# A third buffer for the masked tables, one fewer for the tables and the limits

## The chip, the cores and the metric

The kernel runs on one core of one Trainium2 chip. The metric is the device time of one execution in microseconds (us). An execution covers four graph layers over a batch of 16 graphs of 1,024 nodes with 64 channels.

The engines are named as in the profile: PE (matrix products), DVE (elementwise and reductions), ACT (activations and copies), POOL (here mostly an issuer of transfers) and SP (an issuer of transfers).

## The reference

Every layer is `x = layernorm(x + layer(x, adj))`. What each layer does, cut to what matters:

```python
# layer 0: batch norm over all nodes, then a degree-scaled propagation
Hn = batchnorm(x); d = adj.sum(2)
out0 = leaky_relu(X - sqrt(d) * (adj @ (rsqrt(d) * X)))        # X = Hn @ W + b
# layer 1: 8-head attention; scores = g0 * q.k + g1 * adj; softmax; projection
# layer 2: per node and channel, quantiles over the node's neighbours
adj_  = adj with a unit diagonal
rem   = every second neighbour in node order, of nodes with more than 10 (made symmetric)
nd    = (adj_ > 0) & ~rem                                       # [node, neighbour]
s     = sort over neighbours of where(nd, x, inf)               # per channel
nv    = nd.sum
for tau, w in ((.25, .25), (.5, .5), (.75, .25)):
    pos = tau * (nv - 1); lo, hi = floor(pos), ceil(pos)
    agg += w * (s[lo] + (pos - lo) * (s[hi] - s[lo]))
out2 = relu((x + agg) @ W1 + b1) @ W2 + b2, times a node mask
# layer 3: adj @ (x @ W) + b
```

## The kernel before

The graphs go in pairs, and the outer loop over `p` runs nine times. Round `p` does, in this order:

1. layer 0 of pair `p` (`layer0`, `neighbours`), interleaved with the end of layer 2 and the whole of layer 3 of pair `p-2` (`ends`, `layers23`);
2. attention of pair `p` (`attention`), 64 steps, with the sort of the channels of pair `p-1` beside it (`sorted_words`, from step `BESIDE = 58` on at the latest). At steps 60 to 63 (`TABLES`) `tables(2)` lets DVE make up to two tables `E`, until `EB` of them exist (`first_elements`);
3. the quantile lookup of pair `p-1` (`quantiles`). It takes more than half of the time, and most of the change is in it.

**The lookup.** Each graph has 16 groups of four channels (`G`) and three quantiles (`NQ`). That makes 96 steps for a pair: step `i` is one (graph, group, quantile). Eight steps are a unit (`U8N = 8`). This text writes "step i" for the loop variable `i`, and "the first step of a unit" for `i` divisible by 8. Per group, two tables `E` (bfloat16, 2 KB a partition each) are made by DVE (`words`, `element`), multiplied on PE with the neighbour matrix `ndT` in two halves each (`half_word`), and left by ACT as packed words in `V`. Then, per step:

- `compare(i + 2)`: DVE compares the words with the limits of the quantile (`lim`), result `lt`;
- `one_hot(i + 1)`: PE forms differences of `lt` along the ranks (`lt,dif`), ACT copies them into `oh`;
- `pick(i, 0)` and `pick(i, 1)`: DVE multiplies `V` with `oh` into a masked table `m`, 6 KB a partition. These are the "first pick" and "second pick" of a step;
- `summed(i - 1)`: twelve PE products add the two masked tables of the step before into `wps`. Both are read to nearly the last of the twelve. At the end of a unit, ACT copies `wps` into `wb`, and DVE searches the bit in it over the next six steps (`kth_bit`);
- `distances`, `least_values`, `sum_values` for the step 14 earlier: PE products, which ACT evicts into `vals`, and PE sums into `acc`;
- `more_words` and `more_elements`: the next half words on PE and the next tables on DVE. `more_elements` makes a table only if `made + 1 <= used // 2 + EB`.

**What sets the order.** PE's products of the lookup are chained in the order of the code (`product`, `in_sequence`), and so are DVE's operations that go through `v` (`InOrder`). For everything else a planner of the framework orders each engine's instructions when the program is made, by its own estimate of when inputs and buffers are free. `behind(i)` asks that an instruction be planned after the last `pick`; it is an order in that plan and no wait on the chip. A tile with `bufs=n` waits on the chip until the n-th tile before it has been read for the last time.

**Limits and weights.** `rank_limits` makes `counts` (node degrees `cnt`), `limits(q)` and `weights(t)` of a graph. For the first graph of a pair this is done ahead of the loop. For the second, `SECOND` gives the steps: counts at 26 and 28, weights at 30, 38 and 47, limits at 40, 45 and 46. A limit is one ACT operation (L717) and two DVE operations (L719); a limit of the first graph is last read by `compare` at steps 43, 44 and 45. A weight takes ACT's `kc` (L727) and `nvc` (L728, one buffer) and DVE's L731, L732, L734.

**Memory.** The tables and `lt`, `nvc`, `kc` lie in the pool `qm` at the right end of the on-chip memory; `lim`, `V`, `m` in `qe`, and then `qn`, at the left. The tiles of `layers23` (`tof`, `x2b`, `oT2`, `agg2`) lie in `agg0` at the right end, after the lookup is over.

All of DVE's `v` operations have the profile's line L749 and all chained PE products L933, since a helper records them. They are told apart by their tiles.

Of the kernel before, what the change touches and what calls it, by code (L numbers as in the profile page):

```python
# [13 lines left out]
F32 = mybir.dt.float32  # L14
F16 = mybir.dt.float16
BF = mybir.dt.bfloat16
# [9 lines left out]
P = 128  # L26
N = 1024
# [5 lines left out]
NW = 3  # L33
# [11 lines left out]
MORE = (1, 2, 1, 2, 1, 2, 1, 1)  # L45
SC = 2048.0
VB = 4
EB = 7
LB = 4
LTB = 2  # L50
SECOND = (26, 28, 30, 38, 40, 45, 46, 47)
BESIDE = 58
TABLES = (60, 61, 62, 63)
AHEAD = (10, 12, 15)
# [67 lines left out]
def gnn_kernel(ctx: ExitStack, tc: tile.TileContext, a: dict, out: bass.AP):  # L122
# [105 lines left out]
    def bank(shape, dtype=F32):  # L228
        return ps1.tile(shape, dtype, name="bank")
# [24 lines left out]
    def banks(shape):  # L254
        return two[-1].tile(shape, F32, name="banks")
# [3 lines left out]
    NODES = [P, 4, 2, C]  # L259
# [6 lines left out]
    def over_c(x):  # L266
        return by_half(x)[:, :, :, None].to_broadcast(NODES)

    def over_nodes(x):
        return x[:, None, None, :].to_broadcast(NODES)  # L270
# [25 lines left out]
    def layernorm(dst, y):  # L296

        tiles = norm_tiles()
        norm_stats(tiles, y, range(4))
        norm_apply(tiles, dst, y)  # L300

    def transposed(dst, src, then=lambda i: None):
        ps = bank([P, 512])
        for k in range(4):
            then(nc.tensor.transpose(ps[:, k * P:(k + 1) * P], src[:, k].rearrange("p f c -> p (f c)"), ident))
        nc.scalar.copy(dst, ps)
# [110 lines left out]
    def node_mask(ip, bb):  # L417
        mu = small.tile([P, NB], U8, name="mu", bufs=4)
        nc.sync.dma_start(mu, mask2d[ds(ip * (2 * P) + bb * P, P), :])
        mask_f = small.tile([P, NB], F32, name="mask_f", bufs=4)  # L420
        nc.vector.tensor_copy(mask_f, mu)
        return mask_f
# [276 lines left out]
    def rank_limits(gr, qe, qn, qm, behind):  # L699
# [14 lines left out]
        def limits(q):  # L714

            lim = gr.lim[q] = qe.tile([P, 2, N], U16, name="lim", bufs=LB)
            behind(nc.scalar.activation(lim[:, 0], cnt, AF.Copy, scale=0.25 * (q + 1), bias=-0.25 * (q + 1) - 0.375))  # L717
# [118 lines left out]
    def words(v, pool, g, w, rk, u_w, b_w):  # L836


        sh = [P, 2 * NB, T, 2]
        E = pool.tile([P, NB, P], BF, name="E", bufs=EB)  # L840
        Ev = E.rearrange("p j (h t c) -> p (j h) t c", h=2, t=T)
# [24 lines left out]
    def element(v, qm, gr, g, w):  # L866

        for half, E in enumerate(words(v, qm, gr.bb * G + g, w, rk, u_w, b_w)):
            if not half:
                gr.E.setdefault(g, []).append(E)  # L870
            yield

    def first_elements(qm, graphs):

        for n in range(EB):
            for _ in element(nc.vector, qm, graphs[0], n // EW, n % EW):
# [3 lines left out]
    def quantiles(ip, rk, u_w, b_w, qm, graphs):  # L880
# [12 lines left out]
        with ExitStack() as es:  # L893

            kb, qe, qn = [es.enter_context(tc.tile_pool(name=name, bufs=1, reuse_waits="tile"))
                          for name in ("kb", "qe", "qn")]
            psw = es.enter_context(tc.tile_pool(name="psw", bufs=1, space=PSUM, reuse_waits="tile"))

            def load_matrix(gr):
                gr.ndT = qe.tile([P, NB, N], F8, name="ndT", bufs=2)  # L900
                for k in range(NB):
                    nc.sync.dma_start(gr.ndT[:, k, :].bitcast(U8), nd_d[gr.bb][ds(ip * P, P), k, :])
                gr.bv = qe.tile([P, G, 1], F16, name="bv", bufs=2)
                for c4 in range(4):
                    nc.gpsimd.dma_start(gr.bv[of_channel(c4)],
                                        scratchb[gr.r].rearrange("(g k) (t u) -> k t g u", k=4, u=1)[c4])
# [62 lines left out]
            def pick(u, s, kk):  # L969
                gr, g, q = u.pairs[s]  # L970
                nonlocal picked
                m = qe.tile([P, NW, N], BF, name="m", bufs=2)
                picked = v.tensor_tensor(m, gr.V[g].bitcast(BF),
                                         u.oh[s][:, kk, None, :].to_broadcast([P, NW, N]), ALU.mult)
                u.m.append(m)
# [92 lines left out]
            todo = [(k, w) for k in range(len(groups)) for w in range(EW)]  # L1068
            made, used = EB, 0
            del todo[:made]  # L1070

            def elements():

                nonlocal made
                k, w = todo.pop(0)
                made += 1
                yield from element(v, qm, *groups[k], w)
# [5 lines left out]
            def more_elements(n):  # L1083
                for _ in range(n):
                    if todo and made + 1 <= used // 2 + EB:
                        yield from elements()
# [29 lines left out]
            for i, (u, s) in enumerate(steps):  # L1116
                if i == 3 * NQ:
                    load_matrix(graphs[1])
                if i == SECOND[0]:
                    counts, limits, weights = rank_limits(graphs[1], qe, qn, qm, behind)  # L1120
                if i in SECOND:
                    part, n = ((counts, 0), (counts, 1), (weights, 0), (weights, 1),
                               (limits, 0), (limits, 1), (limits, 2), (weights, 2))[SECOND.index(i)]
                    part(n)
# [61 lines left out]

    hidden = []

    def layers23(agg0, agg1, agg2, tof, ip, bb):
        row = ip * (2 * N) + bb * N  # L1190
        x2 = agg0.tile(NODES, F32, name="x2b")
        oT = agg0.tile([P, 512], F32, name="oT2")
        for f in range(2):
            nc.sync.dma_start(x2[:, :, f, :], x2_d[ds(ip * P, P), 4 * f:4 * f + 4, bb, :])
            nc.sync.dma_start(oT[HALF[f]], x2T_d[ds(ip * P + bb * C, C), f * 512:(f + 1) * 512])
        mask_f = node_mask(ip, bb)
        agg = agg0.tile([P, NU, 512], F32, name="agg2")
        i = nc.scalar.dma_start(agg, agg_d[bb])
        if bb:
            tc.add_manual_dep(i.ins, hidden[0].ins.name, in_order, reason="after the first graph's")  # L1200
        pa = bank([P, 512])
        for u in range(NU):
            for f in range(2):
                nc.tensor.matmul(pa[HALF[f]], tof[HALF[f], u, :], agg[HALF[f], u, :], start=(u == 0),
                                 stop=(u == NU - 1), tile_position=(f * C, f * C))
        nc.vector.tensor_tensor(oT, pa, oT, ALU.add)
        yield
        hp = banks([P, 2, 512])
        hT = agg1.tile([P, N], F32, name="hT", bufs=1)
        for f in range(2):  # L1210
            nc.tensor.matmul(hp[:, f], w1[HALF[f]], oT[HALF[f]], start=True, stop=True)
        hidden[:] = [nc.scalar.activation(hT, hp.rearrange("p f n -> p (f n)"), AF.Relu, bias=b1)]
        yield
        py = bank(NODES)
        for k in range(NB):
            nc.tensor.matmul(py[:, k % 4, k // 4, :], hT[:, k * P:(k + 1) * P], w2, start=True, stop=True)
        y = agg1.tile(NODES, F32, name="y2", bufs=1)
        nc.vector.tensor_tensor(y, py, over_nodes(b2_r), ALU.add)
        nc.vector.tensor_tensor(y, y, over_c(mask_f), ALU.mult)
        nc.vector.tensor_tensor(y, y, x2, ALU.add)  # L1220
        yield
        x3 = agg1.tile(NODES, F32, name="x3")
        layernorm(x3, y)
        yield

        x3T = agg1.tile([P, 512], F32, name="x3T")
        transposed(x3T, x3)
        sup = agg1.tile(NODES, F32, name="sup", bufs=1)
        nc.scalar.copy(sup, by_weights(x3T, w3, C))
        yield  # L1230
        zp = bank([P, 512])
        for k in range(NB):
            at = agg2.tile([P, N], F32, name="at3", bufs=3)
            nc.sync.dma_start(at, adjT2d[ds(row + k * P, P), :])
            propagate(zp, sup, at, k)
            yield
        zT = agg1.tile([P, 512], F32, name="x3T")
        nc.scalar.copy(zT, zp)
        zn = untransposed(zT)
        nc.vector.tensor_tensor(y, zn, over_nodes(b3_r), ALU.add)  # L1240
        nc.vector.tensor_tensor(y, y, x3, ALU.add)
        yield
        layernorm(x3, y)
        for f in range(2):
            nc.sync.dma_start(node_rows(out2d, row, f), x3[:, :, f, :])
# [115 lines left out]
    def ends(ip):  # L1361

        with (tc.tile_pool(name="agg0", bufs=1, reuse_waits="tile", side="right") as agg0,
              tc.tile_pool(name="agg1", bufs=2, reuse_waits="tile", side="right") as agg1,
              tc.tile_pool(name="agg2", bufs=1, reuse_waits="tile", side="right") as agg2):
            tof = agg0.tile([P, NU, C], F32, name="tof")
            nc.scalar.dma_start(tof, a["c_tof"])
            for bb in range(2):
                yield from layers23(agg0, agg1, agg2, tof, ip, bb)

    for p in range(B // 2 + 1):
# [17 lines left out]
        with double_banks(), ExitStack() as es:  # L1391
            last = ends(p - 2) if p >= 2 else iter(())
            if p < B // 2:
                own2 = es.enter_context(tc.tile_pool(name="own2", bufs=1, reuse_waits="tile"))
                x2 = own2.tile([P, NB, 2, C], F32, name="x2")
# [38 lines left out]
            else:  # L1434
                sorted_words()
                tables_of(EB)
        if p >= 1:
# [35 lines left out]
```

## Time and profile before

| What | us |
| --- | --- |
| median of 3 runs | 11,837.91 |
| lowest and highest | 11,832.29 and 11,863.36 |
| the profiled execution's own time | 11,843.83 |
| its span in the trace | 11,842.1 |
| PE busy | 10,550.8 (89%) |
| DVE busy | 10,276.8 (87%) |
| ACT busy | 7,468.6 (63%) |
| POOL busy | 712.4 (6%) |

The mean granted clock of PE in that execution was 0.958. The span runs from the first instruction of the trace to the last; 1.7 us of the profiled time lie outside it. Shares are averages over stages that have different limits. In a group of instructions the columns are: line, engine, operation, out<-in by the program's names, shapes, count; then busy time, mean ns of one, and idle time of the engine just before them with what ended it.

### The profile page before, as it was taken

How to read it: one execution, taken by the hardware profiler on the slowest of the kernel's cores; microseconds unless marked ns; L12 is line 12 of the kernel's file. 1: busy time of each engine (PE TensorE's matmuls, PEld its weight loads, DVE VectorE, ACT ScalarE, POOL GpSimd, SP SyncE). 2: the span in 40 equal slices, each digit the busy share in tenths (PEclk: the TensorE clock that was granted, in tenths of full speed). 3: DMA queues.
4: the chain of work that ended last, by engine and by line, in shares of the span. 5: the costliest groups of instructions: out<-in, count | busy, mean ns of one | idle time of the engine just before them, and what ended most of it. 6: DMA issues, size and time to landing. Idle time of an engine off the chain costs nothing.

```text
span 11842.1 us, 207662 instructions
## 1 busy us (share of the span) xinstructions
PE 10550.8 (89%) x81864; PEld 4573.6 (39%) x82560; DVE 10276.8 (87%) x18374; ACT 7468.6 (63%) x13812; POOL 712.4 (6%) x1212
## 2 busy tenths in 40 slices
PE   7989898998989989898898998989889998983897
PEld 4645232552335423354233542335322453221232
DVE  3588998889988899788997889988999889998996
ACT  5766666666666666566665666656666566661664
POOL 0010000000000000000000000010000100001000
PEclk8989999999999999999999999999999999996999
DMA  2021002210032000310004100041000410002001
GB/s 87 25 100 42 6 6 95 80 29 4 5 110 69 24 4 6 130 52 21 5 6 138 46 18 6 6 143 43 16 5 16 139 43 10 8 24 89 4 5 50
DMA packets 310001, 508.98 MB, mean 43 GB/s; under 512 B 120480, under 2 KB 220192, under 8 KB 306976
## 3 DMA queue, kind: packets, MB, share of 16 engines
q1 hardware_dynamic: 225296, 309.02, 8.3%
q0 software_dynamic: 50688, 99.75, 2.6%
q10 hardware_dynamic: 33040, 86.88, 2.2%
q8 instruction: 649, 10.63, 0.4%
q14 instruction: 328, 2.69, 0.1%
HBM read 379.03 MB, written 116.46 MB: 42 GB/s over the span
## 4 chain that ended last, share of the span: by engine, by line
PE 56%; DVE 27%; ACT 8%; issue 5%; DMA 3%; ACTq 0%; SPq 0%; DVEq 0%; POOL 0%
PE bank L933 19%; DVE m L749 8%; PE banks L549 7%; PE bank L571 7%; PE bank L585 7%; PE acc L933 5%; PE wps L933 3%; DVE S L749 3%; DVE lt L749 3%; ACT vals L1027 2%; DVE U L749 2%; DVE wb L749 2%; PE bank L414 1%; DVE key L1285 1%; PE bank L528 1%
## 5 line engine op out<-in xcount | busy, mean ns | idle before, releaser
L749 DVE TENSOR_TENSOR m<-V,oh 128x3072 bf16<-128x3072 bf16 x1536 | 2671.1, 1750 | 252.0 <-PE wps L933 219.1
L1027 ACT ACTIVATE vals<-bank 128x512 f32<-128x512 f32 x2848 | 1470.5, 602 | 1016.3 <-PE bank L933 1003.1
L933 PE MATMUL bank<-ndT,E 128*128 128x512 fp8e4 x7936 | 1942.2, 389 | 0.0
L556 DVE CUSTOM_DVE_ANT_0 s<-banks,adj 128x1024 f32<-128x1024 f32 x1024 | 1214.0, 1220 | 521.6 <-PE banks L549 516.4
L967 ACT CAST oh<-bank 128x512 f16<-128x512 f32 x3072 | 1591.0, 617 | 20.2 <-PE bank L933 18.6
L575 ACT COPY pT<-bank 128x512 f32<-128x512 f32 x1536 | 802.4, 593 | 812.2 <-PE bank L571 812.1
L564 ACT ACTIVATE s<-s,mx 128x1024 f32<-128x1024 f32 x1024 | 1176.4, 1160 | 98.6 <-DVE mx L556 95.9
L933 PEld LDWEIGHTS <-E 128*128 128x128 bf16 x7936 | 707.8, 99 | 1228.2 <-issue 551.2
L549 PE MATMUL banks<-kT,qT 64*128 64x512 f32 x4096 | 1113.0, 628 | 74.1 <-DVE mx L556 48.5
L571 PEld LDWEIGHTS bank<-ident,s 128*128 128x128 f32 x8192 | 900.6, 143 | 417.8 <-issue 289.7
L571 PE MATMUL bank<-ident,s 128*128 128x128 f32 x8192 | 1034.8, 280 | 8.4 <-ACT s L564 8.1
L933 PE MATMUL bank<-lt,dif 128*128 128x512 bf16 x2424 | 787.4, 383 | 262.9 <-issue 81.4
L585 PE MATMUL bank<-pT,v 128*64 128x256 f32 x8192 | 1003.8, 388 | 0.0
L749 DVE TENSOR_TENSOR lt<-V,lim 128x2048 bf16<-128x2048 uint16 x768 | 934.5, 1217 | 0.0
L933 PE MATMUL wps<-m,tonesb 128*32 128x512 bf16 x9216 | 660.8, 390 | 210.5 <-DVE m L749 208.2
L933 PE MATMUL bank<-oh,bd 64*64 64x512 f16 x11616 | 804.5, 388 | 0.0
L933 PE MATMUL acc<-vals,bonesf 128*32 128x512 f32 x5696 | 801.7, 611 | 2.2 <-ACT vals L1027 2.2
L585 PEld LDWEIGHTS bank<-pT,v 128*64 128x64 f32 x8192 | 548.1, 137 | 312.3 <-issue 47.9
L947 ACT ACTIVATE V<-bank 128x512 uint16<-128x512 f32 x512 | 305.4, 596 | 540.8 <-PE bank L933 476.8
L951 ACT ACTIVATE V<-bank 128x512 uint16<-128x512 f32 x512 | 305.5, 597 | 534.6 <-PE bank L933 533.9
L549 PEld LDWEIGHTS banks<-kT,qT 64*128 64x128 f32 x4096 | 400.1, 190 | 548.7 <-issue 341.2
L933 PE MATMUL bank<-r,pen 32*128 32x512 f16 x5808 | 587.4, 387 | 21.1 <-ACT vals L1027 13.1
(259 smaller groups left out, 14574.6 us busy)
## 6 DMA issues: line engine op xcount, KB each, us to landing
at<-in_adjT SPq DMA_DIRECT2D x256, 512.0 KB, 5.8
masks_d<-mask POOLq DMA_DIRECT2D x440, 128.0 KB, 2.0
mask<-masks_d SPq DMA_DIRECT2D x440, 128.0 KB, 2.1
adj<-in_adj SPq DMA_DIRECT2D x96, 512.0 KB, 6.0
ad<-in_adj ACTq DMA_DIRECT2D x64, 512.0 KB, 7.0
agg_d<-vals POOLq DMA_DIRECT2D x96, 256.0 KB, 2.3
agg<-agg_d ACTq DMA_DIRECT2D x16, 1536.0 KB, 7.6
nd_d<-nd SPq DMA_DIRECT2D x128, 128.0 KB, 2.1
```

The source lines that it names most:

```text
L549: then(nc.tensor.matmul(ss[h][:, hf * 512:(hf + 1) * 512], gr.qk[hp, 0][HALF[h], k * P:(k + 1) * P], gr.qk[hp, 1][HALF[h], hf * 512:(hf + ...
L556: last = nc.vector.tensor_tensor_reduce(s, ss[h], gr.adj[k], -1.0, 3.0e38, ALU.add, ALU.min, mx)
L564: then_act(nc.scalar.activation(s, s, AF.Exp, bias=mx, scale=-1.0, accum_out=sm))
L571: then(nc.tensor.transpose(ps[:, m, :], exps[h][0][:, (4 * mh + m) * P:(4 * mh + m + 1) * P], ident))
L575: then_act(nc.scalar.copy(dst, ps))
L585: then(nc.tensor.matmul(po[HALF[h]], gr.v[:, 4 * mh + m, (2 * hp + h) * C:(2 * hp + h + 1) * C], pT[h][mh][:, m, :], start=(mh == 0 and m ...
L749: i = getattr(nc.vector, name)(*args, **kw)
L933: then(nc.tensor.matmul(*args, **kw))
L947: nc.scalar.activation(gr.V[g][:, 0, cols], ps, AF.Copy, scale=2.0 ** -6, bias=OFF - MAGIC[0] / 64 - 63 / 128)
L951: nc.scalar.activation(gr.V[g][:, 2, cols], ps, AF.Copy, scale=2.0 ** -8, bias=OFF - MAGIC[1] / 256 - 255 / 512)
L967: nc.scalar.copy(u.oh[s][:, kk, cols], ps)
L1027: last = nc.scalar.activation(vals[t], ys[t], AF.Relu)
```

## The change

The masked tables `m` get a third buffer (6 KB a partition more). The tables `E` go from seven buffers to six, and the limits `lim` from four to three (2 KB and 4 KB less). `EB` also bounds how many tables are made ahead. The first limit of the second graph is asked for at step 44 in place of 40. In `ends`, the residual of layer 2 (`x2b`) is allotted ahead of `tof` in place of after it; for the second graph of a pair it is allotted where it was.

```diff
-EB = 7
-LB = 4
+EB = 6
+LB = 3
 LTB = 2
-SECOND = (26, 28, 30, 38, 40, 45, 46, 47)
+SECOND = (26, 28, 30, 38, 44, 45, 46, 47)
...
-                m = qe.tile([P, NW, N], BF, name="m", bufs=2)
+                m = qe.tile([P, NW, N], BF, name="m", bufs=3)
...
-    def layers23(agg0, agg1, agg2, tof, ip, bb):
+    def layers23(agg0, agg1, agg2, x2, tof, ip, bb):
         row = ip * (2 * N) + bb * N
-        x2 = agg0.tile(NODES, F32, name="x2b")
         oT = agg0.tile([P, 512], F32, name="oT2")
...
+            x2b = agg0.tile(NODES, F32, name="x2b")
             tof = agg0.tile([P, NU, C], F32, name="tof")
             nc.scalar.dma_start(tof, a["c_tof"])
             for bb in range(2):
-                yield from layers23(agg0, agg1, agg2, tof, ip, bb)
+                yield from layers23(agg0, agg1, agg2, agg0.tile(NODES, F32, name="x2b") if bb else x2b, tof, ip, bb)
```

## The prediction

> **What bounds it now.** I read the page's busy shares, the busy time by stretch of the second pair's lookup, its waits, then its timeline.
>
> ```profile
> PE 10550.8 (89%) x81864; PEld 4573.6 (39%) x82560; DVE 10276.8 (87%) x18374; ACT 7468.6 (63%) x13812; POOL 712.4 (6%) x1212
> ```
> ```profile
> 2624.00:3407.00 783.00, 695.20 (x5819) 231.94 (x5899) 746.37 (x1089) 519.90 (x989) 40.67 (x75) 0.98 0.02 6
> ```
> ```profile
> 2877.00:2951.00 74.00, 63.58 (x535) 20.91 (x543) 67.49 (x103) 48.80 (x92) 4.86 (x9) 0.95 0.02 6
> 2951.00:3019.00 68.00, 60.27 (x543) 19.92 (x542) 66.77 (x100) 48.23 (x91) 0.56 (x1) 1.00 0.02 5
> 3019.00:3090.00 71.00, 66.75 (x586) 22.34 (x593) 68.92 (x105) 49.40 (x94) 4.88 (x9) 1.00 0.03 6
> ```
>
> Columns: PE, PEld, DVE, ACT, POOL busy, PE's granted clock, DMA. The eight lookups (8 x 783 = 6,264 us) are over half of the span, and DVE works 746.4 of 783 us: a pair can win 36.6 us there at most. The lower rows are three units (steps 32, 40, 48 and on): from step 40 DVE is idle 1 to 2 us a unit.
>
> ```profile
> PE wps L933 <- DVE m L749: 25.6, 21, 6.0
> DVE m L749 <- PE wps L933: 24.2, 17, 4.1
> ACT nvc L728 <- DVE vals L731: 12.6, 3, 6.4
> PE bank L933 <- ACT V L949: 10.4, 8, 5.9
> PE bank L933 <- ACT V L953: 9.0, 8, 4.8
> ACT lim L717 <- DVE lt L749: 2.9, 1, 2.9
> ```
>
> Columns: total, times, longest. The second row is what a third `m` is for. By the timeline, idle time before a pick is 31.4 us a pair, always a first pick: steps 0 (2.03, on ACT's `oh`, stays), 2 (0.46), 26 (0.44), 28 (1.48), 30 to 32 (4.08, 1.76, 1.56), 38 to 40 (3.91, 1.50, 1.02), 56 (1.32), 64 (0.93), 80 (1.32), 86 to 88 (1.06, 3.08, 2.63), 95 (2.18), small rest. But DVE and PE wait for each other in turn, so it matters which of these waits the end passes through.
>
> **The third buffer.** With two, pick (i, 0) waits for sums i-1; with three, pick (i, 1) does, one pick later (1.75 us; 1.67 start to start). At a unit's first step a second wait lies right behind the pick:
>
> ```profile
> 2951.54 1.76 DVE L749 TENSOR_TENSOR m<-V,oh 128x3072 bf16<-128x3072 bf16 x1 [1.02 <-PE wps L933]
> 2953.22 0.42 DVE L749 TENSOR_SCALAR wb<-wb 128x1024 uint16<-128x1024 uint16 x1
> ```
> ```profile
> 2951.61 1.51 ACT L770 CAST wb<-wps 128x1536 bf16<-128x1536 f32 x1
> ```
>
> Sums 39 end at 2951.43, ACT copies until 2953.12, and DVE's search reads the copy at 2953.22. An earlier pick leaves DVE waiting for `wb` until the same moment. So the waits at 30 to 32, 38 to 40, 56, 64, 80 and 86 to 88 run into a wait of the same length: gain 0. At 95 PE ends its sums later than the pick asks for: 0. What remains is step 2 (0.46; PE waits for DVE in steps 6 to 13) and 26 with 28 (1.92): DVE then reaches L731 of step 30's weights earlier, and ACT stands still for that:
>
> ```profile
> 2847.56 2.07 ACT L1027 ACTIVATE vals<-bank 128x512 f32<-128x512 f32 x4
> 2854.94 0.72 ACT L728 ACTIVATE nvc<-cnt,qrow 64x512 f16<-64x512 f16 x1 [5.31 <-DVE vals L731]
> 2855.57 0.57 ACT L951 ACTIVATE V<-bank 128x512 uint16<-128x512 f32 x1
> ```
>
> This `nvc` belongs to step 38's weights; the planner put it ahead of step 29's `V`, and PE idles 4.82 us for that `V`. All of it moves by 1.92. Sum: 0.46 + 1.92 = 2.4 us a pair, 19 in all.
>
> The Trainium skill's page "Perfetto Trace Analysis", section "Optimization Strategy", says that the same gap repeating on the engine that should be saturated can mean too few buffers. By that rule all 31.4 us would go, 8 x 31.4 = 251, and the time would be 11,587. I go by the steps: 21 picks of 192 wait, in clumps that start elsewhere.
>
> **Six tables.** The code's own counts give the same number of tables in each step, one index behind, until step 81; step 82 makes one more (0.68 + 0.68), hidden by step 87's wait of 3.08 (without that cover 8 x 1.36 = 11). The least lead of made over used tables before that falls from 4 to 3. One table (0.68 + 0.42) leaves the end of attention: at 2581.20 it delays a score pass, for which ACT idles 0.67 and PE 0.38. I take 0.4 x 7 = 3 us gained (bounds 0 and 8 x 1.10 = 9).
>
> **Three limits.** Here the change adds a wait on ACT:
>
> ```profile
> 2985.23 2.07 ACT L1027 ACTIVATE vals<-bank 128x512 f32<-128x512 f32 x4 [0.57 <-PE bank L933]
> 2988.12 0.60 ACT L951 ACTIVATE V<-bank 128x512 uint16<-128x512 f32 x1 [0.82 <-PE bank L933]
> 2989.08 2.07 ACT L967 CAST oh<-bank 128x512 f16<-128x512 f32 x4
> 2994.01 1.06 ACT L717 ACTIVATE lim<-cnt 128x1024 uint16<-128x1024 f16 x1 [2.85 <-DVE lt L749]
> 2994.97 1.55 ACT L1027 ACTIVATE vals<-bank 128x512 f32<-128x512 f32 x3
> ```
>
> That is step 46's limit, waiting for `compare` of step 44. With three buffers each limit (44, 45, 46) waits for the `compare` of the step just before it, and it stands in ACT's order earlier than in the code (this one is ahead of step 45's evictions; the `nvc` above sits right behind the DVE operation that frees its buffer). I therefore place each behind the planner's estimate of that `compare`: between evictions and `V` of steps 43, 44, 45. Behind it are queued `V` and the copies `oh`; PE's last `lt,dif` product and its sums wait for `V`, DVE's picks for `oh`.
> - Step 43: evictions end 2980.4, `compare` 2982.84, limit 2984.0; `V` was 2980.68. Sums 43: +3.0.
> - Step 44: `compare` ends 2993.98 (DVE is unmoved), limit 2995.1; `V` was 2988.12. Sums 44: 2991.37 to 2997.4, +6.1.
> - Step 45: oh-copies let `compare` end 0.4 later, 3002.7; limit 3003.8, where the moved `V` would be at 3002.0. Sums 45: 3002.7 to 3008.7, +6.0 (the old stall of 2.26 is part of the old time).
> - Steps 46, 47: PE is at full pace and wins back about 1. Step 48 is a unit's first step: DVE waits for `wb`, 5.0 late.
>
> So +5.0 x 8 = 40. Bounds: +1 a pair if the limits stay behind the `oh` copies, where `compare` is nearly done (one run of 1.06); +10 if they stand ahead of evictions, so that each holds PE up as `nvc` does (4.82 and 5.92, three times, less 2.26 and the slack that steps 45 to 47 have). DVE's two L719 (0.42 each), moved from a waiting step 40 to 44, are inside. 5 is nearest to the rows.
>
> **The residual.** `x2b` was issued on SP at 1974.27 and is first read at 2043.12; 5.1 us to land leave 64 of cover. 0. If its new place is free only after the tail's last products (2028), it still lands in time, ahead of two loads for layers 3 and 0 on SP: at most +1 x 7. `tof` is needed at 2027.4.
>
> **Sum:** -19 - 3 + 40 + 0 = +18. The profiled execution took 11,843.83 (span 11,842.1 + 1.7): 11,862. It lies 5.9 above the median of 11,837.91; against the median, 11,856. A measurement of this kernel can tell about 0.3% (35.5 us) from no change; +18 is below that.
>
> **Rivals.**
> - *The wait goes and nothing takes its place.* For it: 24.2 us in the row above, DVE the busiest engine. Against: the `wb` row. With half of the 29.4 us that aren't step 0's: 11,838 - 118 + 40 - 3 = 11,757. Chance 0.11, faster.
> - *The limits stay behind the `oh` copies.* +1 for +5: 11,838 - 22 + 8 = 11,824. For it: the row at 2994.01. Against: `nvc`. Chance 0.13, same.
> - *Slower: the limits stop ACT ahead of evictions at steps 43 to 45.* +10 a pair: 11,838 - 22 + 80 = 11,896. It decides from 35.5/8 + 2.8 = 7.2 us a pair on. For it: `nvc`'s 5.31 and 6.40 with one freed buffer each. Against: by then each step's evictions are mostly issued. Chance 0.22.
> - *`x2b` holds SP's queue ahead of the loads of `adj` at 1985.85* until 2028: up to 42 x 7 = 294, 12,132. Chance 0.03.
>
> **How the numbers follow.** My own case has 0.51, of which 0.08 (limits at 7 and more) lies above 0.3%. Faster 0.11; same 0.43 + 0.13 = 0.56; slower 0.08 + 0.22 + 0.03 = 0.33. The range 11,800 to 11,925 takes in the second and third rival and the bounds of limits and tables; outside are the first (0.11), `x2b` (0.03) and about 0.05 of tails.
>
> **What would show it.** Right: idle time before first picks falls to step 0's, second picks at 30, 31, 38, 39 wait about 2 less, and DVE's `wb` at 32, 40, 56, 64, 80 waits for ACT's copy, which it doesn't now; three limits a pair wait for `lt`, about 2.4, 3.7 and 1.7 us; the unit of steps 40 to 47 is some 5 us longer, that of 24 to 31 some 2 shorter, the others alike. Wrong: a loop shorter than 775 (first rival), limits that wait under 1 us or units past 48 that change, or a tail that grows between 1972 and 2045.

## The result, and the profile after

The changed kernel took 11,890.14 us (median of 5 runs, 11,882.49 to 11,901.33) where the kernel before took 11,848.47 beside it (5 runs, 11,832.29 to 11,863.36). The ratio is 1.0036, 95% interval 1.0022 to 1.0051: 0.36% slower, inside the range, 34 us from the forecast (41.7 us more than the kernel before, where +18 was forecast). The prediction's own bound for a change that can be told was 0.3%; this lies just beyond it, on the side to which it gave 0.33. The steps of the forecast don't get the credit for the number: two large errors went against each other, and that they nearly cancelled was luck.

First the busy shares of the page after, then the same stretches as before (second pair's lookup; units of steps 32, 40 and 48). Columns as in the prediction.

```profile
PE 10566.1 (89%) x81864; PEld 4593.9 (39%) x82560; DVE 10284.6 (86%) x18374; ACT 7469.7 (63%) x13812; POOL 710.8 (6%) x1212
```
```profile
2644.00:3420.00 776.00, 692.97 (x5816) 230.81 (x5895) 747.97 (x1091) 519.34 (x987) 40.62 (x75) 0.98 0.03 6
2889.00:2962.00 73.00, 64.66 (x543) 21.12 (x547) 66.83 (x101) 48.47 (x93) 4.84 (x9) 0.95 0.02 6
2962.00:3034.00 72.00, 62.09 (x542) 20.23 (x546) 67.87 (x103) 49.02 (x92) 0.56 (x1) 0.98 0.02 5
3034.00:3100.00 66.00, 62.08 (x547) 20.60 (x551) 64.34 (x97) 45.39 (x88) 4.87 (x9) 1.00 0.03 6
```

The work is the same; the lookup is 7 us shorter (776 for 783), and of the units only that of steps 40 to 47 is clearly longer (72 for 68). The row of steps 48 and on that the prediction showed, 71.00, is no whole unit: it runs 5 us past its end. That unit took 66.0 us before (first pick to first pick, 3019.00 to 3084.99), and it does now. The profiled execution as a whole is 57.4 us longer (span 11,899.5 against 11,842.1). Split at the picks and at attention's first and last score products, from the starts in the two traces:

| Stretch | before | after | sum of differences |
| --- | --- | --- | --- |
| lookup, first to last pick, mean of 8 | 782.9 | 776.2 | -53.4 |
| last pick to the next attention, mean of 6 | 201.1 | 218.7 | +105.9 |
| attention, first to last score product, mean of 6 | 411.0 | 410.9 | -0.5 |
| end of attention to first pick, mean of 6 | 44.3 | 43.4 | -5.4 |
| start to the first pick of all | 1187.8 | 1196.2 | +8.4 |
| stretch before the last lookup | 314.2 | 311.0 | -3.2 |
| last pick to the end | 138.8 | 144.4 | +5.6 |

So the lookup won 53 us, where I had a loss of 21 (-19 for the third buffer, +40 for the limits), and the stretch *between* lookups lost 106, where I had 0. The one-time rows need no cause: the start lies between 1187.2 and 1196.2 in the profiles of all twelve kernels of this study, in no order that follows their changes.

**Inside the lookup.** The waits of the second pair's lookup (total, times, longest):

```profile
DVE m L749 <- ACT oh L967: 17.6, 11, 3.5
ACT lim L717 <- DVE lt L749: 6.6, 3, 3.7
ACT nvc L728 <- DVE vals L731: 4.8, 3, 3.9
DVE wb L749 <- ACT wb L770: 4.0, 7, 0.6
DVE m L749 <- PE wps L933: 0.5, 1, 0.5
```

The wait for which the third `m` was built is gone (24.2 to 0.5), and a part of it has moved to `oh` and to `wb`. `lim` grew from 2.9 to 6.6, `nvc` fell from 12.6 to 4.8. ACT at step 29, the place that the prediction showed:

```profile
2866.09 2.07 ACT L1027 ACTIVATE vals<-bank 128x512 f32<-128x512 f32 x4
2868.98 0.60 ACT L951 ACTIVATE V<-bank 128x512 uint16<-128x512 f32 x1 [0.82 <-PE bank L933]
2869.47 0.58 ACT L953 COPY V<-bank 128x512 uint8<-128x512 uint8 x1
2869.94 2.08 ACT L967 CAST oh<-bank 128x512 f16<-128x512 f32 x4
2872.66 1.45 ACT L728 ACTIVATE nvc<-cnt,qrow 64x512 f16<-64x512 f16 x2 [0.65 <-DVE vals L731]
```

Before, `nvc` stood between `vals` and `V` and waited 5.31. Now the planner has it behind `V` and `oh`, and it waits 0.65. Mean over the pairs, step 29 is 4.0 us shorter, step 37 as well, step 27 1.6.

**Between lookups.** SP's, ACT's and PE's rows after the first lookup, whose last pick ends at 1973.82:

```profile
2031.05 0.38 SPq L1193 DMA_DIRECT2D x2b<-x_d  x1
```
```profile
2035.90 0.33 ACTq L1367 DMA_DIRECT2D tof<-in_c_tof  x1
2036.27 0.45 ACTq L1197 DMA_DIRECT2D agg<-agg_d  x1
```
```profile
2048.80 7.96 PE L1203 MATMUL bank<-agg,tof 64*64 64x512 f32 x24 [11.92 <-DMA agg<-agg_d]
```

The same before, where the last pick ended at 1971.96:

```profile
1973.94 0.34 ACTq L1367 DMA_DIRECT2D tof<-in_c_tof  x1
1976.73 0.34 ACTq L1198 DMA_DIRECT2D agg<-agg_d  x1
```
```profile
2027.40 1.07 PE L1204 MATMUL bank<-agg,tof 64*64 64x512 f32 x2
```

Before, the loads left 2.0 and 4.8 us after the last pick, and the first two of these products ran within the tail (in which the `distances` of the last 14 steps follow). Now the loads leave 62 us after it, behind the tail's last evictions on ACT, and PE stands 11.9 us for `agg`; the first graph's whole chain of layers 2 and 3, with layer 0 of the next pair beside it, starts later.

### The profile page after: what moved, and what is told of

Same layout as the page of the kernel before. It is cut to its first block, busy times and chain, and to the rows that moved or that the text cites. A ratio compares the mean times of both kernels' runs of the same rounds, so it can differ in the third digit from the quotient of the medians.

```text
span 11899.5 us, 206953 instructions
## 1 busy us (share of the span) xinstructions
PE 10566.1 (89%) x81864; PEld 4593.9 (39%) x82560; DVE 10284.6 (86%) x18374; ACT 7469.7 (63%) x13812; POOL 710.8 (6%) x1212
## 4 chain that ended last, share of the span: by engine, by line
PE 55%; DVE 27%; ACT 8%; issue 7%; DMA 4%; POOL 0%; ACTq 0%; SPq 0%; DVEq 0%; POOLq 0%
PE bank L933 18%; PE banks L549 7%; DVE m L749 7%; PE bank L571 7%; PE bank L585 7%; PE acc L933 4%; DVE lt L749 3%; PE wps L933 3%; DVE S L749 3%; ACT vals L1027 2%; DVE U L749 2%; DVE wb L749 2%; DMA at<-in_adjT 2%; PE bank L414 1%; DVE E L749 1%
```

## The experiments

Theory A had two halves. *Addresses:* by the tiles' sizes, the left pools grow by 6 - 4 = 2 KB. In the program's memory plan `r64` (of the bit search's result), the last of them, ended before the change at byte 198,272 of a partition, and `agg0` starts at 199,136; 2,048 more bring `r64` to 200,320, which is 1,184 bytes into `agg0`. The tail reads `r64` to its last `distances`, so what lies there is late. *Order:* the third buffer wins by moving `nvc` on ACT, and the limits take back some 4 us a pair. The rivals are in the expectations. "Stretch" is the time from the last pick to the next attention, mean of six; "lookup" is the mean of eight. Ratios are to the kernel before in the same series (median 11,840.94, 11,841.76 and 11,848.28 for e1 to e4, e5 to e8, e9 and e10).

**e1, the residual's move alone.**

```diff
 (kernel before)
-    def layers23(agg0, agg1, agg2, tof, ip, bb):
+    def layers23(agg0, agg1, agg2, x2, tof, ip, bb):
...
-        x2 = agg0.tile(NODES, F32, name="x2b")
         oT = agg0.tile([P, 512], F32, name="oT2")
...
+            x2b = agg0.tile(NODES, F32, name="x2b")
             tof = agg0.tile([P, NU, C], F32, name="tof")
...
-                yield from layers23(agg0, agg1, agg2, tof, ip, bb)
+                yield from layers23(agg0, agg1, agg2, agg0.tile(NODES, F32, name="x2b") if bb else x2b, tof, ip, bb)
```

> The kernel before with only the residual of layer 2 (x2b) allotted ahead of tof. In the changed kernel a pair's lookup is about 7 us shorter than before (775.9 against 782.9, first to last pick), yet the stretch from the end of a lookup to the next attention is 17.6 us longer (218.7 against 201.1, mean of six pairs). Theory A (addresses): that stretch grows because the left pools end 2 KB further up, so that x2b, now lowest in its pool, lies over the buffers of r64, which the lookup's tail reads to its end. Here the left pools end where they did before: 0 us, the stretch stays at 201 and the time at 11,848. Theory B (order): the moved x2b by itself holds back tof and agg: the stretch is 218, and 6 x 17.6 = 106 us are added, 11,950.

Measured: 11,842.59, ratio 1.0002 (0.9993 to 1.0011); stretch 199.4, lookup 783.0. The move costs nothing by itself; theory B falls.

**e2, the change without the third buffer.**

```diff
 (changed kernel)
-                m = qe.tile([P, NW, N], BF, name="m", bufs=3)
+                m = qe.tile([P, NW, N], BF, name="m", bufs=2)
```

> The changed kernel with two masked tables in place of three (tables, limits and residual stay changed). Theory A: the left pools then end below x2b, so the stretch between lookups is 201 as before. The third buffer is what shortened steps 29 and 37 (4.0 us each, the wait of ACT's nvc for DVE's L731 with PE idle behind it), so both stalls are back, and the unit of steps 40 to 47 keeps its loss of about 4.1 from the limits: lookup 783 + 4 = 787, time 11,848 + 8 x 4 = 11,880. Theory C: the shorter steps 29 and 37 come from the fewer tables or the later limits and not from the third buffer: lookup 776, time 11,848 - 55 = 11,793. Theory B: stretch 218 and time 11,880 + 106 = 11,986.

Measured: 11,917.64, ratio 1.0058 (1.0046 to 1.0070); lookup 787.1 as expected, stretch 210.1 where I expected 201. The `nvc` row of its waits, over the whole execution, against 99.1 before and 38.5 after:

```profile
ACT nvc L728 <- DVE vals L731: 101.3, 23, 6.6
```

So it is the third buffer that moved `nvc`: C falls. But the stretch was a miss. SP's rows after the first lookup (last pick 1983.56) show the next overlap:

```profile
1987.91 18.99 SPq L448 DMA_DIRECT2D adj<-in_adj  x7
2008.99 40.47 SPq L347 DMA_DIRECT2D at<-in_adjT  x3
```

Of the three loads of `at` for layer 0, which before were issued 1.9, 4.6 and 6.1 us after that pick, the first now comes after 25 and the other two after 65. Three limits and two masked tables put `vals` 4 KB *lower*, at byte 102,624, under `at`'s third buffer (101,280 to 105,376); the tail uses `vals` to its end. That it is this tile is read from the plan and the late loads; e5 shows only that it is the addresses.

**e3, the collision taken away.** `cnt` (2 KB, last read in the middle of a lookup) gets the last place on the left, above `r64`:

```diff
 (changed kernel)
-            kb, qe, qn = [es.enter_context(tc.tile_pool(name=name, bufs=1, reuse_waits="tile"))
-                          for name in ("kb", "qe", "qn")]
+            kb, qe, qn, qc = [es.enter_context(tc.tile_pool(name=name, bufs=1, reuse_waits="tile"))
+                              for name in ("kb", "qe", "qn", "qc")]
...
-        cnt = qe.tile([P, N], F16, name="cnt")
+        cnt = qc.tile([P, N], F16, name="cnt")
...
```

> The changed kernel with one tile elsewhere: cnt (2 KB, last read before the middle of a lookup) gets a pool of its own above r64, so that x2b lies over cnt and no longer over r64; tables, limits, masked tables and the order of allotment are the changed kernel's. Theory A: the stretch from a lookup to the next attention falls from 218.7 to 201, tof and agg are issued soon after the last pick, and the lookup stays at 776: 11,890 - (6 x 17.6 + 8) = 11,777, or 11,848 - 55 = 11,793 worked out from the kernel before. Theory B (the residual's place, whatever lies under it): stretch 218, time 11,890.

Measured: 11,793.31, ratio 0.9952 (0.9940 to 0.9965); stretch 201.9, lookup 776.4. The loads are back to 3.3 and 6.1 us after the last pick (1971.96):

```profile
1975.26 0.35 ACTq L1367 DMA_DIRECT2D tof<-in_c_tof  x1
1978.05 0.34 ACTq L1197 DMA_DIRECT2D agg<-agg_d  x1
```

Every operation is the changed kernel's, and `x2b` is where it was; `cnt` lies under it in place of `r64`, and `V`, `lim`, `m` and `qn` are 2 KB lower. The other loads of that stretch weren't late in the change: `at` and `adj` left 3.3 to 21 us after the last pick, here 3.3 to 25. That settles the stretch: what lies under `x2b` decides 6 x 16.8 = 101 of its 106 us, the price of 1,184 bytes.

**e4, two buffers for `nvc`.**

```diff
 (kernel before)
-            nvc = qm.tile([P, 512], F16, name="nvc")
+            nvc = qm.tile([P, 512], F16, name="nvc", bufs=2)
```

> The kernel before with two buffers in place of one for nvc, the small tile for which ACT stands still at steps 29 and 37; nothing else changed. As planned, the weights of step 38 then need no wait and those of step 47 are asked for at step 29 in their place: the stall at step 29 should stay, the one at step 37 go. Theory A (what the third masked table won it won by moving nvc behind V on ACT): step 37 is 4 us shorter and step 29 is not, lookup 783 - 4 = 779, time 11,848 - 32 = 11,816. Theory D (the win belongs to DVE's picks, and the nvc stall is only where PE shows it): other waits fill the place, lookup 782 to 783, time 11,848.

Measured: 11,801.95, ratio 0.9963 (0.9949 to 0.9976); lookup 777.6. Step 37 is 4.0 us shorter, steps 38 and 39 together 2.1, and step 47 is 0.7 longer; step 29 is unchanged, with the stall where it was:

```profile
2859.57 0.72 ACT L728 ACTIVATE nvc<-cnt,qrow 64x512 f16<-64x512 f16 x1 [5.32 <-DVE vals L731]
2860.20 0.57 ACT L951 ACTIVATE V<-bank 128x512 uint16<-128x512 f32 x1
```

One run holds both the step that was mended and its control. Little refilled the place (0.7 at step 47, 0.5 in the last unit); D falls.

**e5, e2 with `vals`, `oh`, `r64` and what lies between at their addresses of before.**

```diff
 (e2)
+            unused = qe.tile([P, 2048], F16, name="unused")
+            nc.gpsimd.memset(unused[:, 0:2], 0.0)
             load_matrix(graphs[0])
```

> The kernel with two masked tables, six tables and three limits (e2_two_m) with an unused tile of 4 KB at the start of qe, so that vals, oh, r64 and all behind them lie where they lay in the kernel before. In e2_two_m the lookup was 788 us as expected, but the stretch to the next attention was 210 and not 201; there vals (read through the tail) had moved down 4 KB under layer 0's buffers at, whose second load came 65 us after the last pick and not 5. Theory A (addresses, this time vals under at): with the padding the stretch is 201, the lookup still 4 to 5 us over the one before: 11,841 + 8 x 4.5 = 11,877. Theory E (fewer tables or limits make the stretch longer in some other way): stretch 210, time 11,918.

Measured: 11,859.52, ratio 1.0013 (1.0004 to 1.0022); stretch 198.4, lookup 787.0. An unused 4 KB makes the kernel 58 us faster than e2, and E falls. This is also what six tables and three limits cost without the third buffer: 4.1 us a pair in the lookup (steps 43, 45 and 47: +0.8, +2.3, +1.2), 18 us in all. I expected 36; the stretch is 2.7 us shorter than before, and the profiles of kernels that are alike there lie between 199.4 (e1) and 201.9 (e3), so most of that is their spread.

**e6, the change with the residual back behind `tof`.**

```diff
 (changed kernel)
-    def layers23(agg0, agg1, agg2, x2, tof, ip, bb):
+    def layers23(agg0, agg1, agg2, tof, ip, bb):
         row = ip * (2 * N) + bb * N
+        x2 = agg0.tile(NODES, F32, name="x2b")
...
-            x2b = agg0.tile(NODES, F32, name="x2b")
             tof = agg0.tile([P, NU, C], F32, name="tof")
...
-                yield from layers23(agg0, agg1, agg2, agg0.tile(NODES, F32, name="x2b") if bb else x2b, tof, ip, bb)
+                yield from layers23(agg0, agg1, agg2, tof, ip, bb)
```

> The changed kernel with the residual (x2b) back behind tof, as before; masked tables, tables and limits stay changed. Theory A (addresses): the lowest 2 KB of the pool still lie over r64's last buffer, now with tof in it, and tof, agg and x2b are still issued only after the tail: stretch 218, lookup 776, time 11,890. Theory B (the residual's move costs the stretch): 201 and 11,793. A third outcome, x2b's move having helped: stretch above 219 and time above 11,900.

Measured: 11,877.12, ratio 1.0025 (1.0016 to 1.0034); stretch 217.2, lookup 776.3. Now `tof` itself lies over `r64`, and PE's wait is nearly as long as with `x2b` there (10.0 for 11.9), though `x2b` was issued at 1992.10:

```profile
2042.14 8.22 PE L1204 MATMUL bank<-agg,tof 64*64 64x512 f32 x24 [10.03 <-DMA agg<-agg_d]
```

The residual's place neither causes the loss nor cures it. The intervals of this kernel and of the change overlap.

**e7, three buffers for `nvc`.**

```diff
 (kernel before)
-EB = 7
+EB = 6
...
-            nvc = qm.tile([P, 512], F16, name="nvc")
+            nvc = qm.tile([P, 512], F16, name="nvc", bufs=3)
```

> The kernel before with three buffers for nvc, so that neither step 29 nor step 37 has an nvc behind DVE's L731, and six tables to make room; two masked tables and four limits as before. Two buffers (e4_two_nvc) took 4.0 us off step 37 and 2.1 off steps 38 and 39, 5.7 a pair at the end. Theory A: the stall at step 29 gives as much: lookup 783 - 11.5 = 771, time 11,841 - 8 x 11.5 = 11,749; six tables cost nothing. Theory D (waits refill elsewhere, or six tables hold PE up): no better than two buffers, lookup 777, time 11,802.

Measured: 11,724.49, ratio 0.9898 (0.9885 to 0.9912); lookup 770.9, stretch 199.6. Both stalls are gone, and six tables cost nothing that shows. The time is 25 lower than expected; the lookups explain 8 x 12.0 = 96 of the 117; of the rest, 6 x 1.5 lies between lookups and 6 x 1.7 in attention, both within what these vary by between profiles of kernels that are alike there (199.4 to 201.9 and 409.1 to 412.0).

**e8, the limits (and the last weights) one step later**, on e3:

```diff
 (e3)
-SECOND = (26, 28, 30, 38, 44, 45, 46, 47)
+SECOND = (26, 28, 30, 38, 45, 46, 47, 48)
```

> e3_counts_last (the changed kernel with the collision at the boundary taken away) with the second graph's limits asked for at steps 45, 46 and 47 in place of 44, 45 and 46, and its last weights at 48. Each limit is then asked for one step after the compare that frees its buffer, in place of in the same step. Theory A (the unit of steps 40 to 47 is 4.1 us longer because ACT stands at a limit for that compare): the unit loses under 1 us, time 11,793 - 8 x 4 = 11,761. Theory F (DVE's part of the limits, or the order around them, costs it): unit still 3 to 5 us longer, time 11,793 or more.

Measured: 11,750.60, ratio 0.9922 (0.9909 to 0.9936); lookup 772.2. The unit of steps 40 to 47 is 0.8 us longer than before, in place of 4.1, and one limit of three still waits:

```profile
2970.30 1.06 ACT L717 ACTIVATE lim<-cnt 128x1024 uint16<-128x1024 f16 x1
2979.96 1.06 ACT L717 ACTIVATE lim<-cnt 128x1024 uint16<-128x1024 f16 x1 [2.25 <-DVE lt L749]
```

F falls: 3.3 of the 4.1 us were ACT's waits at the limits.

**e9, `nvc` planned one set of weights later, no buffer changed.**

```diff
 (kernel before)
-                nc.scalar.activation(nvc[b], x, AF.Identity, bias=qrow[b, t, 4:5])
+                behind(nc.scalar.activation(nvc[b], x, AF.Identity, bias=qrow[b, t, 4:5]))
```

> The kernel before with one word changed in weights: nvc, like kc beside it, is planned behind the last pick (behind), so that ACT makes it at the step that asks for it (30, 38, 47) and not one set of weights ahead, in front of V, where it stands for DVE's L731. No buffer is added or taken, every address is that of before. Theory A (the order of nvc and V on ACT is what steps 29 and 37 lose): both stalls go as with three nvc buffers (lookup 12.3 us shorter, 11,724 measured there), less 0.7 for an nvc that now stands beside kc at each of steps 29 and 37: lookup 783 - 11 = 772, time 11,842 - 8 x 11 = 11,754 or up to 30 lower. Theory D (buffers and what is made ahead of need): steps 29 and 37 as before, 11,842.

Measured: 11,767.13, ratio 0.9934 (0.9919 to 0.9948); lookup 772.6. ACT at step 29 has no `nvc` between `vals` and `V` any more:

```profile
2842.88 2.06 ACT L1027 ACTIVATE vals<-bank 128x512 f32<-128x512 f32 x4
2845.77 0.60 ACT L951 ACTIVATE V<-bank 128x512 uint16<-128x512 f32 x1 [0.82 <-PE bank L933]
```

With every address and every count of buffers as before, an order on ACT alone is worth 10.3 us a pair: more than all that the change won in the lookup.

**e10, all of it**: e8 with e9's line.

> e8_limits_later (third masked table, six tables, three limits one step later, cnt on top) with nvc planned behind the last pick as in e9_nvc_behind. Beside e9_nvc_behind this tells what the third masked table is worth once it is not needed to move nvc. If what it wins by itself is the first units (1.2 us by step 24) and the few first picks late in a pair (steps 85, 86, 94: up to 3), less what the limits still cost: 3 us a pair, 24 us below e9_nvc_behind. If all it won was nvc's place: equal to e9_nvc_behind within 10 us. If all 31.4 - 16 = 15 us of idle time before picks counted: 120 us below.

Measured: 11,724.86, ratio 0.9895 (0.9883 to 0.9908); lookup 768.4, the shortest of all, 4.2 below e9's. The waits of the second pair's lookup:

```profile
PE wps L933 <- DVE m L749: 23.8, 21, 6.0
DVE m L749 <- ACT oh L967: 11.0, 8, 2.8
DVE wb L749 <- ACT wb L770: 3.1, 6, 0.6
```

The lookups account for 34 of the 42 us to e9. As a whole it ties with e7, which has two masked tables and nothing moved at the boundary (0.9898): either is some 120 us faster than the kernel before and 165 faster than the change.

## Why the prediction was right in its number and wrong in its steps

- **The residual: 0, bounds +1 x 7.** This step failed, and it is the largest term: +106. I followed `x2b`, and for `x2b` alone the reasoning holds (it landed at 2033 to 2035 and is read at 2066). What I didn't follow is the address. I added up what the buffers cost on the left (+6 - 4 KB) nowhere, although the change named those sizes, so I didn't see that something must then lie over `r64`. And the prediction gave `tof` and `agg` no term at all (it says of `tof` only when it is needed); both stood on ACT behind the tail's last evictions where `x2b` or `tof` lay over `r64` (the change, e6), and not where `x2b` lay over `cnt` (e3). Why the planner puts them there isn't shown: a rule that what is allotted later also comes later doesn't fit e6, where `x2b`, allotted behind the late `tof`, left 39 us ahead of it. The rival that I had for this place (`x2b` holding up SP's loads of `adj`) had the right place and the wrong victim (and its 12,132 leaves out the +18 of the other terms): `adj` was issued from 1978.6 on, and `agg` was late.
- **The third buffer: -2.4 a pair.** The first place was right (step 29), the mechanism there wasn't, and the size is wrong by a factor of over four: the change less e5 is 776.2 - 787.0 = -10.8 a pair, 86 us. I had found the row (`nvc` ahead of `V`, PE idle 4.82) and let "all of it move by 1.92", as if ACT's order were fixed. It isn't: with the third buffer the planner puts `nvc` behind `V`, and without it (e2) the stalls are back; that its estimates moved with the earlier pick is the likely reason, and not shown. What I had as a shift was a removal. The unit of steps 24 to 31 is 6.2 shorter for the forecast 2, that of steps 32 to 39 1.8 for none. With `nvc` out of the way (e10 less e9) the third buffer, with what the limits and the six tables still cost in it, is worth 4.2 a pair. The forecast 2.4 is the right order of size for that, but not its places: 2.4 of the 4.2 lie in the units from step 48 on, where I had 0.
- **The waits that I set to 0.** Right in part. Over the whole execution DVE's wait for ACT's `wb` went from 27.5 us in 8 places to 70.9 in 65, as forecast for the first steps of units. Wrong in that these waits are shorter than those that went (0.56 each in the second pair) and that the units from step 48 on are together 1.5 shorter for the forecast 0; and in that idle time before first picks did not fall to step 0's: 31.5 to 18.2 a pair, since `oh` became the late one. Second picks, which by the forecast should have come to wait, do so once in the second pair (0.46, step 46).
- **The limits: +5.0 a pair.** Right: +4.1 in the unit of steps 40 to 47 in the change, +4.6 in e5, and e8 took 3.3 of the 4.1 away. The waits came as 3.7, 1.75 and 1.1 (6.6 in all) for the forecast 2.4, 3.7 and 1.7. In step 43 the limit stood among the evictions, not behind them; the third rival's order occurred once in three, without its price. No term rests on the row of steps 48 and on that was taken for a unit.
- **Six tables: -3 in all.** The stretch from attention to the first pick is 0.9 shorter (5.4 in six); within the bounds of 0 to 1.10 each.
- **The rule.** The Trainium skill, "Perfetto Trace Analysis", section "Optimization Strategy", says that a gap that repeats on the engine that should be saturated can mean too few buffers. Read so, the gap before the picks would have been worth 251 us. The buffer alone won 86, more than half of it through `nvc` (10.8 a pair, of which e10 less e9 leaves 4.2, or by estimate some 5 with the limits' 0.8 added). Too few buffers would describe `nvc` too, whose stall repeats in every pair and which a second and third buffer removed (e4, e7), though it sits on ACT, busy 63%; and e9 removed it without any buffer.

Of what I had named as signs of error, "a tail that grows between 1972 and 2045" is what came; "a loop shorter than 775" just didn't (776.2), and no unit from step 48 on changed by more than 0.6.

The first rival had the right sign for the lookup: at other addresses the change is faster (e3: 11,793), though 36 us short of that rival's 11,757, and more than half of the gain came through `nvc`, which that rival doesn't name.

## What to carry to other kernels

When buffer counts change, add up the bytes and look at what then lies over what at the next stage's boundary: a tile of the next stage over one that is read last in this one can cost more than the buffer wins (106 us for 53 here), and a tile that dies early, put last, cured it here. When an engine stands at an instruction that isn't urgent, with urgent ones queued behind it, move that instruction before adding buffers. And where a planner sets the order, do not price an edit by shifting the old order: say what each stall is queued behind, and let the range hold the case that this order changes.

## What was not expected of the hardware

Nothing but a small thing: `agg` took 12.4 us from issue to landing in the change (2036.27 to 2048.66) and 9.1 before (1976.73 to 1985.84). Both times it goes out among other loads (`tof`, `x2b` and `at`); after the tail there are more of them, and whether these cost the 3.3 us was not tried.
